# Unequal chunks of a field pair in one VectorE multiply, padded with zeros of W

## The chip, the cores and the metric

The kernel runs on 1 core of one Trainium2 chip. The metric is the device time of one execution in microseconds (us), the median of several runs.

## The reference

Each of 4096 rows holds 32 fields of 64 numbers. For every pair of fields i < j, field i is multiplied by a 64 x 64 matrix of its own and the result by field j, element by element:

```python
i_idx, j_idx = np.triu_indices(32, k=1)          # 496 pairs
vdotw = jnp.einsum('bpd,pde->bpe', inputs[:, i_idx, :], W)
inter = vdotw * inputs[:, j_idx, :]              # (4096, 496, 64), fp32
return inter.reshape(B, -1)                      # 4096 x 31744, 520 MB
```

The input is 34 MB and W 8 MB; the output is 520 MB.

## The kernel before

The 4096 rows go in 32 row tiles of 128. Field i needs (31 - i) x 64 columns of W, so the fields' widths fall by 64 from one to the next. Two neighbouring fields form a pair p, one on partitions 0 to 63 and the other on 64 to 127. Each pair goes in chunks of 512 columns of each field; TensorE makes the two products in PSUM, VectorE multiplies them by x and writes into a ring in SBUF, from which five stores per row tile go out.

```python
for c0 in range(0, width[2 * p], BANK):                  # BANK = 512
    pm = psum.tile([P, 2, BANK], F32, tag="ps", ...)     # 4 places of two banks
    n = [max(0, min(BANK, width[2 * p + h] - c0)) for h in range(2)]
    ...                                                  # a matmul per field, n[h] columns
    if n[0] == n[1]:                                     # equal halves: one instruction
        nc.vector.tensor_tensor(runs(osb, o[0], o[1], n[0]), pm[:, :, : n[0]],
                                runs(xt, xj[0], xj[1], n[0]), ALU.mult)
    else:                                                # ragged: one per field
        for h in range(2):
            if n[h]:
                nc.vector.tensor_tensor(osb[:, o[h] : o[h] + n[h]], ...)
...
nc.sync.dma_start(out=out[ts(t, P), o0 : o0 + store_w[s]], in_=osb)   # end of a group of pairs
```

`runs(tile, a, b, n)` is an access pattern on a tile: two runs of n columns that begin at columns a and b.

## Time and profile before

| | before |
|---|---|
| time | 1341.25 us (1340.96 to 1341.39, 3 runs) |
| VectorE busy | 1177.4 us, 88%, 1664 instructions |
| TensorE busy | 1151.0 us, 86% |
| transfer engines, share of the span | 98.8% |
| VectorE waits for a store to leave the ring | 93.0 us |

"Busy" counts the time in which at least one instruction of the engine is recorded as running. The transfers' share is averaged over 16 engines.

### The profile page before, as it was taken

The numbers are of one execution on the slowest core, as the hardware profiler recorded it, in microseconds if no ns is written. First come the engines' busy times: TensorE is split into PE (matmuls) and PEld (weight loads), VectorE is DVE, ScalarE is ACT, GpSimd is POOL, SyncE is SP. The second block draws the span as 40 slices with busy tenths as digits, with TensorE's granted clock in tenths as the row PEclk, the third lists the DMA queues.
The fourth block names the chain that finished last, engine by engine and source line by source line (L and its number), as shares of the span: only waits on it lengthen the run. The fifth ranks groups of instructions, "written<-read, shape, count | busy, mean of one in ns | idle before, by whom it ended". The sixth has DMA issues, their size and how long they took to land.

```text
span 1339.7 us, 13755 instructions
## 1 busy us (share of the span) xinstructions
PE 1151.0 (86%) x5376; PEld 548.7 (41%) x5376; DVE 1177.4 (88%) x1664; ACT 66.1 (5%) x65; POOL 0.7 (0%) x6
## 2 busy tenths in 40 slices
PE   7998889888898888988888978889798897888992
PEld 3444344443343443443433534444344443444441
DVE  6999889888899988989888989899898997898993
ACT  1000000000000000000000000000000000000000
POOL 0000000000000000000000000000000000000000
PEclk9999889999999999989999899899898998998996
DMA  9999999999999999999999999999999999999996
GB/s 392 426 431 434 429 431 429 427 427 434 426 434 430 422 422 430 422 424 429 415 426 424 426 426 404 415 420 431 428 420 408 431 427 431 416 424 420 422 429 264
DMA packets 30017, 562.93 MB, mean 420 GB/s; under 512 B 3456, under 2 KB 3840, under 8 KB 5376
## 3 DMA queue, kind: packets, MB, share of 16 engines
q1 hardware_dynamic: 25344, 528.49, 92.6%
q10 hardware_dynamic: 4608, 33.56, 6.0%
q8 instruction: 42, 0.69, 0.2%
q14 instruction: 23, 0.19, 0.0%
HBM read 41.94 MB, written 520.09 MB: 420 GB/s over the span
## 4 chain that ended last, share of the span: by engine, by line
DMA 54%; DVE 23%; PE 11%; issue 9%; DVEq 0%
DMA out_dram<-ring 54%; DVE ring L130 15%; PE pm L120 9%; DVE ring L139 9%; PE pt L80 2%; DMA x<-in_x_dram 1%; DVEq L130 0%; DVEq L177 0%
## 5 line engine op out<-in xcount | busy, mean ns | idle before, releaser
L120 PE MATMUL pm<-w,xT 64*128 64x512 f32 (+7 forms) x4864 | 1083.2, 559 | 158.3 <-DVE ring L130 140.1
L130 DVE TENSOR_TENSOR ring<-pm,x 128x1024 f32<-128x1024 f32 x768 | 904.0, 1217 | 138.4 <-DMA out_dram<-ring 93.0
L120 PEld LDWEIGHTS pm<-w,xT 64*128 64x128 f32 x4864 | 487.7, 194 | 720.1 <-DVE ring L130 451.3
L139 DVE TENSOR_TENSOR ring<-pm,x 128x448 f32<-128x448 f32 (+6 forms) x896 | 330.2, 415 | 3.6 <-PE pm L120 2.9
L81 ACT COPY xT<-pt 128x1024 f32<-128x1024 f32 x64 | 64.8, 1012 | 1194.6 <-PE pt L80 1194.6
L80 PE MATMUL pt<-ident,x 128*128 128x128 f32 x512 | 76.5, 297 | 8.5 <-DMA x<-in_x_dram 8.5
L80 PEld LDWEIGHTS pt<-ident,x 128*128 128x128 f32 x512 | 61.0, 152 | 48.9 <-issue 35.3
L81 ACT ACT_TABLE_LOAD x1 | 1.3, 1283 | 1.7 <-PEq L173 1.7
masks.py:199 POOL TENSOR_SCALAR_AFFINE_SELECT ident<-ident 128x128 f32<-128x128 f32 x1 | 0.3, 292 | 0.1
masks.py:197 POOL MEMSET ident<- 128x128 f32 x1 | 0.2, 204 | 0.3 <-POOLq L173 0.3
L173 POOL MEMSET const-bfloat16-1.0<- 128x1 bf16 x1 | 0.1, 101 | 0.0
L173 POOL MEMSET const-uint8-127<- 128x1 uint8 x1 | 0.1, 101 | 0.0
L173 POOL MEMSET const-float32-0.0<- 128x1 f32 x1 | 0.1, 98 | 0.2 <-issue 0.2
L173 POOL MEMSET const-float32-1.0<- 128x1 f32 x1 | 0.1, 98 | 0.0
## 6 DMA issues: line engine op xcount, KB each, us to landing
out_dram<-ring SPq DMA_DIRECT2D x32, 3776.0 KB, 22.8
out_dram<-ring SPq DMA_DIRECT2D x32, 3264.0 KB, 21.8
out_dram<-ring SPq DMA_DIRECT2D x32, 3168.0 KB, 22.4
out_dram<-ring SPq DMA_DIRECT2D x32, 2912.0 KB, 22.3
out_dram<-ring SPq DMA_DIRECT2D x32, 2752.0 KB, 22.1
x<-in_x_dram ACTq DMA_DIRECT2D x32, 1024.0 KB, 14.2
w<-in_w_dram SPq DMA_DIRECT2D x1, 992.0 KB, 7.4
w<-in_w_dram SPq DMA_DIRECT2D x1, 928.0 KB, 11.7
```

What stands on the lines that cost most here:

```text
L80: nc.tensor.transpose(pt[:, ts(c, P)], xt[:, ts(n * g + c, P)], ident)
L81: nc.scalar.copy(xT[:, ts(g, 2 * BANK)], pt)
L120: nc.tensor.matmul(pm[:, h, : n[h]], xT[h * D : (h + 1) * D, ts(p, P)], w_sb[p][h * D : (h + 1) * D, c0 : c0 + n[h]], start=True, stop=True,)
L130: nc.vector.tensor_tensor(runs(osb, o[0], o[1], n[0]), pm[:, :, : n[0]], runs(xt, xj[0], xj[1], n[0]), ALU.mult,)
L139: nc.vector.tensor_tensor(osb[:, o[h] : o[h] + n[h]], pm[:, h, : n[h]], xt[:, xj[h] : xj[h] + n[h]], ALU.mult,)
L173: nc = bacc.Bacc("TRN2", target_bir_lowering=False, num_devices=1)
```

## The change

Its intent is to save VectorE instructions: the last chunk of a pair, where one field has 64 columns more than the other, becomes one instruction of two equal runs instead of two. The odd field's run is filled up with 64 columns of W that are zero anyway. The 64 zeros land in the ring where the next pair's results start and are overwritten by them; only where that would leave the store's place do two instructions remain. PSUM becomes a hand-made ring of banks, and x two fixed buffers with 64 zero columns behind. Core of the diff:

```diff
-                    if n[0] == n[1]:
+                    if n[1] > half - BANK and o[1] + n[0] <= store_w[s]:
                         nc.vector.tensor_tensor(
                             runs(osb, o[0], o[1], n[0]),
-                            pm[:, :, : n[0]],
+                            runs(pm, 0, half, n[0]),
                             runs(xt, xj[0], xj[1], n[0]),
                             ALU.mult,
                         )
...
-                    pm = psum.tile([P, 2, BANK], F32, tag="ps", name=f"pm_{t}_{p}_{c0}")
+                    half = -(-n[0] // BANK) * BANK
+                    pm = take_banks(2 * half // BANK)
...
-                                w_sb[p][h * D : (h + 1) * D, c0 : c0 + n[h]],
+                                w_sb[p][h * D : (h + 1) * D, c0 + b0 : c0 + b1],   # b1 = min(b0 + BANK, n[0])
...
+    xbuf = [const.tile([P, (F + 1) * D], F32, ...) for b in range(2)]              # 64 zeros at the end
```

More of the change, by code (lines that the diff above doesn't have):

```diff
@@ L14 @@
 BANK = 512
+BANKS = 8
+CHUNK = BANK
 STORES = [[0, 1], [2, 3], [4, 5], [6, 7, 8], [9, 10, 11, 12, 13, 14, 15]]
@@ L57, in pair_bilinear_kernel @@
     const = ctx.enter_context(tc.tile_pool(name="const", bufs=1))
-    xpool = ctx.enter_context(tc.tile_pool(name="x", bufs=2))
     xtpool = ctx.enter_context(tc.tile_pool(name="xT", bufs=2))
-    psum = ctx.enter_context(tc.tile_pool(name="ps", bufs=4, space=bass.MemoryType.PSUM))
+    psum = ctx.enter_context(tc.tile_pool(name="ps", bufs=1, space=bass.MemoryType.PSUM))
     ident = const.tile([P, P], F32, tag="ident", name="ident")
@@ L68, in runs, with take_banks @@
         return bass.AP(ap.tensor, ap.offset, [list(ap.ap[0]), [b - a, 2], list(ap.ap[1])])
+    xbuf = [const.tile([P, (F + 1) * D], F32, tag=f"x{b}", name=f"x{b}") for b in range(2)]
+    for xb in xbuf:
+        nc.gpsimd.memset(xb[:, F * D :], 0.0)
     def load_x(t):
-        xt = xpool.tile([P, F * D], F32, tag="x", name=f"x_{t}")
-        nc.scalar.dma_start(out=xt, in_=x[ts(t, P), :])
-        return xt
+        xt = xbuf[t % 2]
+        nc.scalar.dma_start(out=xt[:, : F * D], in_=x[ts(t, P), :])
+        return xt
+    pring = psum.tile([P, BANKS * BANK], F32, tag="pring", name="pring")
+    bank = 0
+    def take_banks(n):
+        nonlocal bank
+        if bank + n > BANKS:
+            bank = 0
+        got = pring[:, bank * BANK : (bank + n) * BANK]
+        bank = (bank + n) % BANKS
+        return got
     def transpose_x(xT, t, xt, g):
         n = 2 * BANK // P
-        pt = psum.tile([P, 2 * BANK], F32, tag="ps", name=f"pt_{t}_{g}")
+        pt = take_banks(2)
         for c in range(n):
@@ L114, in pair_bilinear_kernel @@
                     transpose_x(xTs[t + 1], t + 1, xs[t + 1], PREFETCH_AT.index(p))
-                for c0 in range(0, width[2 * p], BANK):
-                    pm = psum.tile([P, 2, BANK], F32, tag="ps", name=f"pm_{t}_{p}_{c0}")
-                    n = [max(0, min(BANK, width[2 * p + h] - c0)) for h in range(2)]
-                    for h in range(2):
-                        if n[h]:
-                            nc.tensor.matmul(
-                                pm[:, h, : n[h]],
-                                xT[h * D : (h + 1) * D, ts(p, P)],
-                                w_sb[p][h * D : (h + 1) * D, c0 : c0 + n[h]],
-                                start=True,
-                                stop=True,
-                            )
+                for c0 in range(0, width[2 * p], CHUNK):
+                    n = [max(0, min(CHUNK, width[2 * p + h] - c0)) for h in range(2)]
+                    half = -(-n[0] // BANK) * BANK
+                    pm = take_banks(2 * half // BANK)
+                    for b0 in range(0, n[0], BANK):
+                        b1 = min(b0 + BANK, n[0])
+                        for h in range(2):
+                            if b0 < n[h]:
+                                nc.tensor.matmul(
+                                    pm[:, h * half + b0 : h * half + b1],
+                                    xT[h * D : (h + 1) * D, ts(p, P)],
+                                    w_sb[p][h * D : (h + 1) * D, c0 + b0 : c0 + b1],
+                                    start=True,
+                                    stop=True,
+                                )
                     o = [off[2 * p + h] - o0 + c0 for h in range(2)]
                     xj = [(2 * p + h + 1) * D + c0 for h in range(2)]
-                    if n[0] == n[1]:
+                    if n[1] > half - BANK and o[1] + n[0] <= store_w[s]:
                         nc.vector.tensor_tensor(
                             runs(osb, o[0], o[1], n[0]),
-                            pm[:, :, : n[0]],
+                            runs(pm, 0, half, n[0]),
                             runs(xt, xj[0], xj[1], n[0]),
@@ L140, in pair_bilinear_kernel @@
                                     osb[:, o[h] : o[h] + n[h]],
-                                    pm[:, h, : n[h]],
+                                    pm[:, h * half : h * half + n[h]],
                                     xt[:, xj[h] : xj[h] + n[h]],
```

## The prediction

> **What bounds the kernel now.** I read the page first, then the waits, the chain, stretches of the span, and the timeline of VectorE. The page shows three things that look busy: PE, DVE and the transfers.
>
> ```profile
> PE 1151.0 (86%) x5376; PEld 548.7 (41%) x5376; DVE 1177.4 (88%) x1664; ACT 66.1 (5%) x65; POOL 0.7 (0%) x6
> ...
> DMA  9999999999999999999999999999999999999996
> ...
> q1 hardware_dynamic: 25344, 528.49, 92.6%
> q10 hardware_dynamic: 4608, 33.56, 6.0%
> ...
> DMA 54%; DVE 23%; PE 11%; issue 9%; DVEq 0%
> ```
>
> VectorE at 88% and the 16 transfer engines at 92.6 + 6.0 + 0.2 = 98.8% of the whole span: the transfers are the ones without room. The chain agrees, since 54% of it is a store of the output ring. Who waits for whom says the same from the other side (columns: waiter, released by, us in total, times, longest):
>
> ```profile
> DVE ring L130 <- DMA out_dram<-ring: 93.0, 53, 3.3
> DVE ring L130 <- PE pm L120: 45.4, 52, 13.2
> ```
>
> So VectorE stands still for 93.0 us until a store has left the ring. Of the 45.4 us for TensorE, 13.2 are the start, before any product exists. Then stretches of the span (the last two columns are the transfer engines' share and GB/s):
>
> ```profile
> 100.00:500.00 400.00, 349.54 (x1634) 168.28 (x1634) 356.96 (x509) 20.24 (x20) 0.00 (x0) 0.95 1.00 429
> 500.00:900.00 400.00, 351.63 (x1646) 166.65 (x1642) 358.53 (x502) 20.24 (x20) 0.00 (x0) 0.96 0.99 422
> 900.00:1300.00 400.00, 350.14 (x1633) 166.57 (x1630) 360.38 (x510) 18.22 (x18) 0.00 (x0) 0.95 1.00 424
> ...
> 1326.00:1328.00 2.00, 0.00 (x0) 0.00 (x0) 0.00 (x0) 0.00 (x0) 0.00 (x0) 0.50 0.88 375
> 1328.00:1330.00 2.00, 0.00 (x0) 0.00 (x0) 0.00 (x0) 0.00 (x0) 0.00 (x0) 0.50 0.06 25
> 1330.00:1334.00 4.00, 0.00 (x0) 0.00 (x0) 0.00 (x0) 0.00 (x0) 0.00 (x0) 0.50 0.06 24
> 1334.00:1339.70 5.70, 0.00 (x0) 0.00 (x0) 0.00 (x0) 0.00 (x0) 0.00 (x0) 0.50 0.05 20
> ```
>
> The share is 0.99 to 1.00 all the way. The end is telling: from 1328 us to 1339.7 us the mean share is 0.05 to 0.06, and 0.06 x 16 = 1. One of the 16 engines is about 11 us behind the other fifteen and ends the kernel alone. It moves 11.7 us x about 23 GB/s = 270 KB there, while its sixteenth of the last store (5824 columns x 128 rows x 4 B = 2.98 MB) is 186 KB. So it reaches the last store only some time after 1330 us, although that store was issued at 1319.5 us. The last store's issue could come about 10 us later without moving the end. What bounds the kernel is thus the work of the slowest transfer engine, not VectorE.
>
> **What the Trainium skill says.** "DMA: Bandwidth & Descriptors", section "Where 436 GB/s comes from", puts the ceiling of the 16 ports at 435.2 GB/s. The trace agrees: 429, 422 and 424 GB/s above are 97 to 99% of it. "VectorE: DVE Perf Modes", section "The perf-mode tier table (the rule you actually need)", leaves an fp32 product of two tensors in its plain mode, with any PSUM operand; one element per cycle at the 0.96 GHz of that page is 1.04 ns. The trace agrees: from 64 to 448 columns the instruction goes from 215 to 617 ns, (617 - 215) / 384 = 1.05 ns a column, with a fixed part of 215 - 67 = 148 ns. Section "The DRAIN you can't avoid" of that page says that a semaphore between VectorE instructions costs nothing extra. Here I doubt it, because of this:
>
> ```profile
> 59.63 2.35 DVE L130 TENSOR_TENSOR ring<-pm,x 128x1024 f32<-128x1024 f32 x2
> 61.89 0.55 DVE L139 TENSOR_TENSOR ring<-pm,x 128x192 f32<-128x192 f32 x2
> 62.35 3.48 DVE L130 TENSOR_TENSOR ring<-pm,x 128x1024 f32<-128x1024 f32 x3
> 65.75 0.22 DVE L139 TENSOR_TENSOR ring<-pm,x 128x64 f32<-128x64 f32 x1
> ```
>
> Two instructions of 1024 columns begin at 59.63 and the next begins at 61.89, so one takes 1.13 us from start to start, though its recorded length is 1.217 us. Neighbours overlap by 84 ns: the record of one runs past the start of the next. "Perfetto Trace Analysis", section "DVE / Act Engine Instruction (TENSOR_ADD, Activation, etc)", explains it: the recorded window runs up to the acknowledged write, and the semaphore spreads only after that. An instruction that has to wait for its neighbour loses the overlap.
>
> **The change part by part.**
>
> *VectorE instructions.* A row tile has 24 chunks of two equal halves and 16 ragged ones: 4 with only the even field (64 columns) and 12 with two unequal parts. Of these 12, three end a store (pairs 1, 5 and 8), where the padded run would pass the end of the store's place in the ring, and stay two instructions. Nine are merged (pairs 0, 2, 4, 6, 9, 10, 12, 13, 14). So 9 x 32 = 288 instructions go, from 1664 to 1376.
>
> *What one merge saves.* From start to start an instruction costs 148 - 84 = 64 ns plus 1.05 ns a column. Away goes 64 ns; in come 64 columns of zeros, 64 x 1.05 = 67 ns. The trace lets me check it: the pair 192 + 128 above takes 62.35 - 61.89 = 0.46 us, and one instruction of 384 would take 64 + 403 = 467 ns. The saving is nil. By recorded lengths it would look like 148 - 67 = 81 ns each, 23 us in all, but most of that lies under the neighbour.
>
> *What one merge adds.* In the compiled order of the changed kernel VectorE waits for its own semaphore 288 times, each time for the instruction directly ahead: the merged instruction writes 64 zeros where the next pair's results begin, so the next instruction, which overwrites them, must wait for it. In the kernel before there are 803 such waits, but for writes of an earlier turn of the ring, finished long ago, so they hold nothing up. A new wait costs the 84 ns of overlap plus the semaphore. For the latter I take the 50 ns that TensorE needs after VectorE in this trace (a VectorE instruction ending at 17.64 us releases a weight load at 17.69 us). 134 ns x 288 = 39 us; at 200 ns each it would be 58 us. Counted as busy time, where the lost overlap shows and the gap does not, DVE goes from 1177 to about 1177 + 288 x (67 - 64 + 84) / 1000 = 1202 us, on fewer instructions.
>
> *TensorE.* The odd half of all 12 two-part chunks and of none else grows by 64 columns. Two passes over 512 columns follow each other every 0.43 us (weight loads at 12.51, 12.94 and 13.37 us), 0.42 ns a column, so 12 x 32 x 2 passes x 27 ns = 21 us at most, if nothing overlaps. TensorE's own pace is about 0.86 us for a 1024-column chunk against VectorE's 1.13, so this stays hidden.
>
> *Buffers.* PSUM becomes one hand-made ring of eight banks, taken two at a time: four places as before. x gets two fixed buffers with 64 columns of zeros behind, as many as before, and each load still waits for the same readers. GpSimd writes the zeros once (two small writes ahead of the identity's last step, a few tenths of a us), while x arrives only at 8.3 us. The stores are the same 160, of the same sizes.
>
> *The sum on the path.* VectorE needs 39 us more (21 to 58), against 93.0 us in which it waits for stores. Per tile of 1340 / 32 = 42 us that is 1.2 us against 2.9. The wait for the ring shrinks to about 54 us, and the transfers see nothing of it. At the end the last group holds five merged chunks, so the last store is issued about 5 x 0.134 = 0.7 us later, against 10 us of room. Net: 0 us.
>
> **The rivals.**
>
> *A: VectorE sets the pace, and fewer instructions help.* For it: 88% busy, 23% of the chain. Against it: 93.0 us of waiting for stores, and the nil balance above. Even the 23 us of recorded lengths would only lengthen the wait for the ring. At most about 1335 us.
>
> *B: the new waits are dearer and VectorE becomes the bound.* They would have to cost over 93 / 288 = 0.32 us each to use up the room on average; 2% (27 us) more needs 120 / 288 = 0.42 us. For it: the room is not evenly spread, and I have not seen such a wait in this trace. Against it: three stores are under way at a time (each takes about 22 us to land, one is issued every 8), so a short lag drains a backlog and not the engines. I give this a few chances in a hundred; 1350 to 1370 us.
>
> *C: the transfers themselves change pace*, because VectorE reaches the ring at other times. The rate already wanders between 404 and 434 GB/s from slice to slice, yet three runs lie within 0.5 us of each other. A us or two either way.
>
> **Range and chances.** The middle is the time before, 1341 us. Below it, C and a rest of A make 1336 us; above it, C and the start of B make 1347 us. Faster by over 2% means under 1314 us. The 528.49 + 33.56 = 562 MB at the 429 GB/s of the best stretch take 1310 us, and with the 12 us of the lone engine at the end, that is out of reach: 0.01. Slower by over 2% needs B in full: 0.03. Same: 0.96.
>
> **What would show it.** Right: 1376 VectorE instructions; DVE busy up to about 1200 us in spite of that; the wait of VectorE for stores down from 93 to 35 to 75 us; short gaps of some tens of ns after merged chunks; the transfers still at 0.99 to 1.00 and one engine alone at the end. The step on the new waits is wrong if DVE busy stays at 1177 or falls and the wait for stores stays at 90 or grows: then the semaphore is free, as the skill says. The whole is wrong if the share of the transfers falls clearly below 0.98 in the middle stretches, with VectorE busy or held by its own waits there, or if the time falls by more than 6 us: then VectorE did set the pace.

## The result, and the profile after

| | before | after |
|---|---|---|
| time | 1341.36 us (1340.96 to 1341.43, 6 runs) | 1339.73 us (1339.52 to 1339.92, 6 runs) |
| VectorE busy | 1177.4 us, 1664 instructions | 1199.8 us, 1376 instructions |
| VectorE waits for stores | 93.0 us | 55.9 us |
| VectorE waits for TensorE | 48.3 us | 30.7 us |

The ratio of after to before is 0.9988, with a 95% interval of 0.9975 to 1.0001: the same. (Ratios here are the mean time of one kernel's fast runs over that of the other's in the same rounds, so not quite the ratio of the medians quoted.) 288 VectorE instructions went, 17%, and VectorE is busy for longer than before. From the page of the changed kernel, first the engines, then the transfers:

```profile
PE 1142.4 (85%) x5376; PEld 511.0 (38%) x5376; DVE 1199.8 (90%) x1376; ACT 66.1 (5%) x65; POOL 0.9 (0%) x8
...
DMA  9999999999999999999999999999999999999996
...
q1 hardware_dynamic: 25344, 528.49, 92.7%
q10 hardware_dynamic: 4608, 33.56, 6.0%
q8 instruction: 42, 0.69, 0.2%
q14 instruction: 18, 0.15, 0.0%
```

The transfers' row is digit for digit that of before. In the list of waits of the changed kernel (waiter, released by, us, times, longest) the wait for stores has shrunk, and that for TensorE too:

```profile
DVE ring L155 <- DMA out_dram<-ring: 55.9, 35, 3.0
DVE ring L155 <- PE pring L145: 30.7, 27, 12.9
```

The end of the changed kernel by stretches (last two columns: transfer share, GB/s):

```profile
1326.00:1328.00 2.00, 0.00 (x0) 0.00 (x0) 0.00 (x0) 0.00 (x0) 0.00 (x0) 0.50 0.09 37
1328.00:1330.00 2.00, 0.00 (x0) 0.00 (x0) 0.00 (x0) 0.00 (x0) 0.00 (x0) 0.50 0.09 37
1330.00:1334.00 4.00, 0.00 (x0) 0.00 (x0) 0.00 (x0) 0.00 (x0) 0.00 (x0) 0.50 0.05 23
1334.00:1338.10 4.10, 0.00 (x0) 0.00 (x0) 0.00 (x0) 0.00 (x0) 0.00 (x0) 0.50 0.04 17
```

As before, about one engine of sixteen is still at work in the last 12 us. The trace also keeps the times of every packet, which no view prints, though not its engine. They show it directly: after the last packet of the others, packets follow each other end to end for 9.9 us (10.3 in the kernel before). Followed back in this way, that engine has no pause over 0.02 us from 93 us on, and brings the last packet of every store, in both kernels: it is the one that bounds them. What the change did to VectorE shows at the end of a row tile, where pairs 11 to 15 follow each other. VectorE's timeline before (start, us, instruction; a row can hold several of one line, named by the first):

```profile
85.72 2.53 DVE L139 TENSOR_TENSOR ring<-pm,x 128x64 f32<-128x64 f32 x8
88.17 1.22 DVE L130 TENSOR_TENSOR ring<-pm,x 128x1024 f32<-128x1024 f32 x1
```

and after:

```profile
86.75 0.21 DVE L164 TENSOR_TENSOR ring<-pring,x 128x64 f32<-128x64 f32 x1
86.89 2.67 DVE L155 TENSOR_TENSOR ring<-pring,x 128x896 f32<-128x896 f32 x3
89.66 0.23 DVE L164 TENSOR_TENSOR ring<-pring,x 128x64 f32<-128x64 f32 x1
89.81 1.22 DVE L155 TENSOR_TENSOR ring<-pring,x 128x1024 f32<-128x1024 f32 x1
```

Before, eight instructions take 88.17 - 85.72 = 2.45 us until the next begins. After, five take 89.81 - 86.75 = 3.06 us. The five hold three of the new waits, so 0.6 / 3 = 0.20 us each. One is visible by itself: the three merged instructions end at 86.89 + 2.67 = 89.56, and the next one starts at 89.66, 0.10 us later. Where there is no such wait, as at 86.75 + 0.21 = 86.96, the next one has started at 86.89, 0.07 us before.

### The profile page after: what moved, and what is told of

Read it like the earlier page. It is cut to its first block, busy times and chain, and to the rows that moved or that the text cites. A ratio compares the mean times of both kernels' runs of the same rounds, so it can differ in the third digit from the quotient of the medians.

```text
span 1338.1 us, 13157 instructions
## 1 busy us (share of the span) xinstructions
PE 1142.4 (85%) x5376; PEld 511.0 (38%) x5376; DVE 1199.8 (90%) x1376; ACT 66.1 (5%) x65; POOL 0.9 (0%) x8
## 4 chain that ended last, share of the span: by engine, by line
DMA 41%; DVE 39%; PE 16%; issue 2%; DVEq 0%
DMA out_dram<-ring 41%; DVE ring L155 35%; PE pring L145 13%; DVE ring L164 4%; PE pring L102 3%; DMA x<-in_x_dram 1%; DVEq L155 0%; DVEq L164 0%
## 5 line engine op out<-in xcount | busy, mean ns | idle before, releaser
L155 DVE TENSOR_TENSOR ring<-pring,x 128x1024 f32<-128x1024 f32 (+3 forms) x1056 | 1115.8, 1102 | 115.3 <-DMA out_dram<-ring 55.9
L145 PE MATMUL pring<-w,xT 64*128 64x512 f32 (+4 forms) x4864 | 1077.5, 560 | 165.7 <-DVE ring L155 161.4
L145 PEld LDWEIGHTS pring<-w,xT 64*128 64x128 f32 x4864 | 452.5, 189 | 758.6 <-DVE ring L155 601.3
L103 ACT COPY xT<-pring 128x1024 f32<-128x1024 f32 x64 | 64.8, 1013 | 1193.8 <-PE pring L102 1193.8
L164 DVE TENSOR_TENSOR ring<-pring,x 128x64 f32<-128x64 f32 (+3 forms) x320 | 114.5, 383 | 3.7 <-DVE ring L155 0.5
L102 PE MATMUL pring<-ident,x 128*128 128x128 f32 x512 | 73.6, 290 | 8.5 <-DMA x<-in_x_dram 8.5
L102 PEld LDWEIGHTS pring<-ident,x 128*128 128x128 f32 x512 | 58.5, 147 | 46.9 <-issue 36.9
```

What stands on the lines that cost most here:

```text
L102: nc.tensor.transpose(pt[:, ts(c, P)], xt[:, ts(n * g + c, P)], ident)
L103: nc.scalar.copy(xT[:, ts(g, 2 * BANK)], pt)
L145: nc.tensor.matmul(pm[:, h * half + b0 : h * half + b1], xT[h * D : (h + 1) * D, ts(p, P)], w_sb[p][h * D : (h + 1) * D, c0 + b0 : c0 + b1 ...
L155: nc.vector.tensor_tensor(runs(osb, o[0], o[1], n[0]), runs(pm, 0, half, n[0]), runs(xt, xj[0], xj[1], n[0]), ALU.mult,)
L164: nc.vector.tensor_tensor(osb[:, o[h] : o[h] + n[h]], pm[:, h * half : h * half + n[h]], xt[:, xj[h] : xj[h] + n[h]], ALU.mult,)
```

## The experiments

The theory: the transfers set the time; the change makes VectorE slower by 288 waits for the neighbour, and this disappears in VectorE's wait for stores. The rivals: VectorE's pace counts and fewer instructions help; or the wait is free; or the slowdown of VectorE comes from the zeros.

### 1. No room to hide in: half of each store

```diff
-nc.sync.dma_start(out=out[ts(t, P), o0 : o0 + store_w[s]], in_=osb)
+nc.sync.dma_start(out=out[ts(t, P), o0 : o0 + store_w[s] // 2], in_=osb[:, : store_w[s] // 2])
```

The result is wrong: half of the output is never written. The same edit in the kernel before:

> The kernel before, storing only the first half of each store's columns (wrong on purpose), so that the transfers need about half the time and VectorE sets the pace. Theory: about 1177 us of VectorE work, 30 to 45 us of waits for TensorE and some 15 us of ends: 1215 to 1250 us, no wait for stores to speak of. Rival (the transfers' rate is not what bounds, something per store is): stays above 1300 us.

in the changed kernel:

> The changed kernel with the same half stores. Theory: with nothing to hide behind, the 288 new waits at about 180 ns make it about 50 us (30 to 55) slower than the kernel before with half stores. Rival (fewer instructions save their recorded fixed part): 20 us faster. Rival (no cost and no saving): equal.

and in the changed kernel with the order of experiment 2:

> Half stores and the ragged chunk first: only 96 of the 288 waits are for the neighbour. Theory: two thirds of the loss come back, so 12 to 22 us slower than the kernel before with half stores. If the loss of the changed kernel has another cause (the zeros' 64 columns, TensorE's wider halves), it stays at the same loss as the changed kernel with half stores.

| half stores | time | against before |
|---|---|---|
| before | 1195.07 us | |
| changed | 1247.27 us | +52.2 us |
| changed, ragged chunk first | 1211.21 us | +16.1 us |

The first lies a little under its range, the others within theirs. From the pages of the first and the second:

```profile
PE 1101.4 (92%) x5376; PEld 519.5 (43%) x5376; DVE 1168.4 (98%) x1664; ACT 66.1 (6%) x65; POOL 0.7 (0%) x6
```
```profile
PE 1115.5 (90%) x5376; PEld 496.4 (40%) x5376; DVE 1195.6 (96%) x1376; ACT 66.1 (5%) x65; POOL 0.9 (0%) x8
```

VectorE is busy for 98% and 96% of the span, and neither kernel has a wait for stores left. So with whole stores it is the transfers that hold the kernel at 1341 us; VectorE could do it in about 1195. And the change, taken by itself, costs 52.2 us: 52.2 / 288 = 181 ns for each new wait. The trace agrees: with half stores the gap behind a merged multiply is 104 ns in the median of the 288, where neighbours without a wait overlap by about 80 ns, 184 ns together. (181 is a net figure: VectorE also waits 10 us less for TensorE, 13.4 against 23.8 us, and small lengthenings make up for that, such as 1217 against 1211 ns for each of the 768 multiplies of 1024 columns.) Of the rivals, the one with savings (20 us faster) and the one with none are out. That 192 of 288 waits less give back 36.1 of the 52.2 us, 69% for 67% of the waits, leaves about nothing for the zeros or for TensorE's wider halves, since those are the same in both.

### 2. The waits alone: ragged chunk first

```diff
-for c0 in range(0, width[2 * p], CHUNK):
+for c0 in reversed(range(0, width[2 * p], CHUNK)):
```

The stores are whole. The zeros are written first and overwritten some instructions later, so for 192 of the 288 the instruction waited for is not the one directly ahead.

> The changed kernel with the ragged chunk of each pair computed first: 192 of the 288 waits for the instruction directly ahead become waits for an instruction two or more back, 96 stay. Theory (transfers bound the kernel; a new wait costs VectorE 84 ns of overlap and a gap of about 100 ns): DVE busy falls from 1199.8 to about 1184 us, the gaps of VectorE from about 28 to about 10 us, its wait for stores rises from 56 to 75 to 90 us, and the time stays at 1339 to 1341 us. Rival (VectorE's pace still counts): the time falls by 10 us or more. Rival (semaphore is free): DVE busy stays at 1200 us.

Measured: 1340.32 us (ratio 0.9994, interval 0.9981 to 1.0006). DVE busy is 1186.8 us, down from 1199.8. VectorE's waits for stores, one row for each of its two source lines:

```profile
DVE ring L155 <- DMA out_dram<-ring: 69.3, 30, 4.2
DVE ring L164 <- DMA out_dram<-ring: 22.8, 20, 1.9
```

Together 92.1 us, as in the kernel before and just above the range. VectorE gained most of its loss back, and all of it went into waiting. The rival in which VectorE's pace counts wanted 10 us; it is out.

### 3. How much room is left: more VectorE work

First try, which missed: small multiplies of x by x at the head of each pair.

```diff
+for _ in range(1 if p % 2 == 0 else 0):          # 8 per row tile; in the other run 2 for every pair, 32
+    nc.vector.tensor_tensor(spare[:, e : e + D], xt[:, :D], xt[:, D : 2 * D], ALU.mult)
```

> The changed kernel with 8 more VectorE instructions of 64 columns per row tile, 256 in all, about 131 ns each: 33 us of VectorE work. Theory (about 80 us of room left, since the half-store kernel runs at 1247 us): the time stays within 2 us of the changed kernel, and VectorE's wait for stores falls from 56 to 15 to 40 us. Rival (room is used up): 15 us or more longer.

> The same with 32 per row tile, 1024 in all: 134 us of VectorE work. Theory: the room of about 80 us is used up, VectorE sets the pace, 1365 to 1400 us, its wait for stores is under 10 us, and the transfers' share falls to about 0.97. Rival (VectorE never matters at these sizes): 1340 us.

They took 1603.51 and 1661.28 us, far beyond both theories. In the waits of the run with 8 stands why:

```profile
DVE spare L142 <- DMA x<-in_x_dram: 325.2, 32, 11.7
```

These instructions, which need nothing but x, had been moved ahead in compiling. In the trace all eight of the next row tile stand within nine instructions near the start of the present one, and VectorE waits there, 10 us a tile, for a load that nobody else needs yet. The runs say nothing of the room. Second try, reading the product just made, so that none can be moved:

```diff
+for _ in range(1 if c0 == 0 and p % 2 == 0 else 0):   # behind the chunk's own multiply; 2 for every pair in the other run
+    nc.vector.tensor_tensor(spare[:, e : e + D], pm[:, :D], xt[:, :D], ALU.mult)
```

> The changed kernel with 8 more VectorE instructions of 64 columns per row tile (256 in all), this time reading the product just made, so that none can be moved ahead of it: 34 us of work, less 12 us for 64 neighbour waits that now have an instruction in between, 22 us net. Theory (room of 80 us or so): the time stays at 1339 to 1342 us (256 more instructions to fetch are 0.6 us of it) and VectorE's wait for stores falls from 56 to 25 to 50 us. Rival (the room is used up): 1360 us or more.

> The same with 32 per row tile, 1024 in all: 134 us of work, less 18 us for 96 neighbour waits with an instruction in between, 116 us net. Theory: over the room; the half-store kernel's 1247 us + 116 us + about 10 us for the longer last store make 1373 us (1360 to 1390), the wait for stores is under 10 us and the transfers' share falls below 0.98. Rival (VectorE is hidden at this size too): 1342 us.

With 8: 1340.66 us, and the wait for stores fell from 55.9 to 37.6 us, as expected:

```profile
DVE ring L157 <- DMA out_dram<-ring: 37.6, 25, 2.5
```

With 32: 1364.41 us, within the range, 24.7 us more than the changed kernel for 116 us of net work. (116 us is the estimate made before the run; VectorE's busy time rose by 118.9 us.) Its page:

```profile
PE 1165.2 (86%) x5376; PEld 495.3 (36%) x5376; DVE 1318.7 (97%) x2400; ACT 66.1 (5%) x65; POOL 0.9 (0%) x8
```

VectorE now sets the pace, and no wait for stores is left in its list. The transfers' share did not fall as low as expected, 0.98 to 0.99 in the middle stretches. So the changed kernel has about 116 - 24.7 = 91 us of room, and before the change it was about 91 + 52 = 143 us.

### 4. What the last engine does: more instructions to fetch

The changed kernel has 598 fewer instructions in all (13157 against 13755; the other 310 are mostly small semaphore steps of VectorE), and instructions are fetched by transfers too. Could that be its 1.6 us? Tiny writes on the idle GpSimd add instructions and no data:

```diff
+for i in range(4800):
+    nc.gpsimd.memset(spare[:, i % 64 : i % 64 + 1], 0.0)
```

> The changed kernel with 4800 tiny writes on the idle GpSimd at the start, whose only cost to the others is that their instructions have to be fetched. Theory (the lone engine that ends the kernel is the one that also fetches instructions; instruction packets of 16 KB for 256 instructions mean 64 B each; 307 KB more at the 27 GB/s of one engine): 11 us longer (8 to 14), so 1348 to 1354 us, and the lone engine's stretch at the end grows or stays. Rival (fetches are spread over the 16 engines): at most 1 us longer. Rival (the lone engine is behind for another reason and fetches fall on another one): 0 to 3 us.

with half stores:

> Half stores and the 4800 tiny GpSimd writes. Control for the run with the same writes and whole stores (14 us longer). Theory (the 14 us come through the transfer engine that fetches): with half stores that engine has room, so 1247 us as without the writes, within 3 us. Rival (GpSimd's writes slow VectorE or the start): about 14 us longer again, 1261 us.

and only 600 of them:

> The changed kernel with 600 tiny GpSimd writes, which bring the count of instructions (13157) back to that of the kernel before (13755). Theory (the 1.6 us by which the changed kernel is shorter are the fetches of 598 fewer instructions, at 14.1 us per 4800): 1.8 us longer than the changed kernel, 1341.0 to 1342.0 us, the time before. Rival (the 1.6 us are chance or come from elsewhere): 1339.5 to 1340.2 us.

Measured: 1353.87 us with 4800 (14.1 us more than the changed kernel, at the upper end of the range), and 1248.53 us with half stores (1.3 us more than without the writes, so GpSimd does not slow VectorE). The fetch queue with 4800:

```profile
q14 instruction: 56, 0.46, 0.1%
```

against 18 packets and 0.15 MB in the changed kernel. 0.31 MB spread over 16 engines would take 0.31 MB / 430 GB/s = 0.7 us; on one engine, a sixteenth of that rate, 11.5 us. 14.1 us is too much for an even spreading. It does not show that the fetches fall on the very engine that ends the kernel, as the theory has it, and the packet records speak against that. The delay does arise while the writes run (until 190 us), and from 284 us on it stays at about 14.1 us. But two engines lag in that stretch, at 202 us by 10.4 and 15.0 us behind the middle one of the sixteen, and at most a dozen of this queue's 53 packets after 20 us fit between the packets of the engine that ends the kernel. The stretch at the end in which it is alone, expected to grow or stay, fell from 9.9 to 7.4 us. What slows that engine stays open.

The run with 600 took 1340.29 us, 0.6 us more than the changed kernel where 1.8 were expected, outside both ranges. But it was a poor test. Its writes are all over at 24 us; its stores are 1.6 us late at 78 us, only 0.5 us at 160 us and 0.4 us at the end, so most of an early delay is made up. The kernel before falls behind the changed one evenly instead: 0.5 us at 489 us, 1.0 at 818, 1.6 at the end. Writes spread over the whole kernel were not run. The packet records rule out one reading: of this queue's 23 packets in the kernel before and 18 in the changed one, four in each belong to the engine that ends last, so the five more are not on it. Its output packets take longer, 1232.5 us in all against 1230.8, and why is not shown. With an interval that holds 1, I leave the 1.6 us open.

### 5. Fewer still: chunks of 1024

```diff
-CHUNK = BANK
+CHUNK = 2 * BANK
```

> The changed kernel with chunks of 1024 columns of each field: 928 VectorE instructions, and about 500 fewer to fetch in all. Theory (VectorE is hidden; only the instructions fetched touch the engine that ends last, 32 KB at 27 GB/s): 1 us less than the changed kernel, 1338 to 1340 us. Rival (VectorE's count of instructions counts): 20 us less. Rival (two PSUM places in place of four stop TensorE and VectorE from overlapping, and it shows): over 1350 us.

1519.14 us, 13% longer, with only 928 VectorE instructions: the second rival. A chunk takes four of eight banks, which leaves two places in PSUM instead of four, one to fill and one to empty. VectorE's two rows of waits for TensorE:

```profile
DVE ring L155 <- PE pring L145: 239.0, 230, 15.1
DVE ring L164 <- PE pring L145: 79.8, 32, 3.5
```

Together 319 us, against 31 in the changed kernel. Nothing is left of the room of 91 us. The changed kernel is within 0.2% of the one before, and the reordered one lies between.

## Why the prediction was right

The time alone tests little of the working: any cost to VectorE up to the room of about 140 us would have left it where it was. What tests it are the half-store runs and the waits.

- **The bound.** Transfers, not VectorE: shown by the half stores (1341 to 1195 us), by VectorE work that came and went at constant time (experiments 2 and 3), and by the one engine without a pause in the packet records. Right.
- **The room of 93 us.** Too small: it was about 143 us. I counted only the waits for stores. Part of the waits for TensorE is room as well (I take it, without a run of its own, that both engines have to start up again after a wait for the ring): after the start they were 45.4 - 13.2 = 32 us, and 23.8 - 14.6 = 9 us with half stores. The rest are the shorter end with half stores and slightly shorter VectorE instructions.
- **A merge saves nothing, 64 ns against 67.** Right within the runs: the 52.2 us are 181 ns for each wait, and the timeline accounts for 0.17 to 0.20 us of wait alone.
- **A merge costs 134 ns of wait.** The direction was right, the size was off by a third: 181 ns. The overlap of 84 ns was right. The semaphore was the mis-sized term: I took 50 ns from VectorE's release of TensorE; VectorE's release of itself leaves a gap of 104 ns, not "some tens of ns". The sum was 39 us (21 to 58) and is 52.2.
- **DVE busy about 1202 us, wait for stores about 54 us.** 1199.8 and 55.9. The second is partly luck: the cost was 13 us more than I had, and the wait for TensorE took up 48.3 - 30.7 = 18 us of it.
- **TensorE's wider halves stay hidden.** Right: 1142.4 us busy against 1151.0.
- **The end.** One engine alone near the end, for 10.3 us before and 9.9 us after. In the kernel before its packets of the last store begin at 1331.5 us, as worked out ("some time after 1330 us"). Rival C, "a us or two either way", is the size of what remains, 1.6 us; its cause is open.

## What to carry to other kernels

Before saving instructions on an engine, look at what it waits for: an engine that is 88% busy can still have 10% of the span to spare, and then neither a gain nor a loss on it reaches the time. Fewer instructions are not less work: a merge that makes neighbours overlap in memory turns a pipelined stream into one with waits, here 181 ns each against 64 ns saved, which the 67 ns of zeros already used up, and the page shows that as more busy time on fewer instructions. If such a merge is wanted, put another instruction between the write and the overwrite; that gave back two thirds of the loss here, for one word in a loop.

## What the Trainium skill lacked or had wrong

- "VectorE: DVE Perf Modes", section "The DRAIN you can't avoid", says, from a measurement of eight `tensor_copy`, that a semaphore between VectorE instructions costs nothing extra. Here a wait for the instruction directly ahead cost 181 ns (52.2 us for 288, half-store runs): a gap of 0.10 us in place of an overlap of 0.08 us in the record.
- "Runtime: NRT & Kernel Launch", section "Instruction fetch mechanics", calls the cost of a fetch mostly hidden. It does not say what more instructions can cost in a kernel bound by transfers: 4800 on an idle engine, with 0.31 MB more to fetch, cost 14.1 us with whole stores and 1.3 us with half stores. How much of this is the fetch is not shown.
- "DMA: Bandwidth & Descriptors", section "Latency and other measured facts", says that two of the 16 transfer engines are usually slower, but takes this for specific to descriptors made by software, and gives no size. Here, on queues that the profile calls hardware_dynamic and with equal shares of the output, one engine ended 10 us after the others in both kernels.
